# Queries of two units from a copy of the pixels, keys of two units in the other step, bias coefficients laid out contiguously

## The chip, the cores and the metric

The kernel runs on one NeuronCore of one Trainium2 chip. The metric is the device time of one execution in microseconds; the time given is the median of three runs. The kernel before takes 3091.45 us (3091.44 to 3092.21).

## The reference

The input is x, two images of 128 channels and 256 x 256 pixels, in fp32. Two layers follow each other, each adding its result to its input after a group normalisation.

Layer 0 is halo attention. Pixels are grouped in windows of 8 x 8; each window's 64 queries look at the 12 x 12 pixels around it. There are four heads of 32 channels:

```python
qkv = jnp.einsum('bchw,oc->bohw', x, W_qkv)
q = q * SCALE
attn = jnp.einsum('bnd,bmd->bnm', q, k)
attn = attn + rel_pos_emb(q, rel_height, rel_width) + FIXED_MASK
attn = jax.nn.softmax(attn, axis=-1)
out = jnp.einsum('bnm,bmd->bnd', attn, v)
return jnp.einsum('bchw,oc->bohw', out, W_out)
```

The fixed mask puts minus infinity on every pair of query and key whose row or column distance has the wrong parity. What is left is four separate attentions per window: 16 queries (4 x 4) against 36 keys (6 x 6) of one parity of rows and one of columns. The position terms are dot products of a query with a table, one per row distance and one per column distance. They are linear in the pixel, so they can be computed from the normalised pixels with the tables folded into the query weights.

Layer 1 is a pair of convolutions whose results are multiplied; the change doesn't touch it, except that one of its buffers is declared with the shape of a buffer of layer 0.

## The kernel before

Layer 0 works in strips of eight image rows, 32 strips an image, 64 in all. A strip k has two units u = 2k and 2k + 1, one for each parity r of rows; a unit holds both parities c of columns, 16 pairs of windows each. 128 units run one after the other in `attention_fast` (L548 to L597).

The normalised pixels of a strip are in `xn[k % 2]` (two buffers), by row parity, pair of windows, column parity and then a cell of 10 x 6 pixels (j rows, i columns) that belongs to one window of the pair and the halo. The name `by_cell` gives this view. `inner(k, r, c, lo, hi)` takes rows 1 to 8 of each cell and columns lo to hi of it: four floats, then a step to the next cell row, six floats further.

There is also a copy of the pixels by place, `xq`: one buffer, with the layout place column t2, half of the pairs, place row t1, r, pair n, c, e. POOL fills it in `by_place` (L331), eight copies a strip: four in the even unit of the strip before and four in the odd one. Only the bias coefficients read it.

What a unit does, in the order in which the code emits it:

- `normalise(k + 1)`, in even units: POOL copies the old columns (L312), VectorE normalises the new ones in four instructions (L321) and copies edges (L326, L327).
- `by_place` for half of strip k + 1's columns (L335, POOL), `old_keys(u + 1)` (L346, POOL): key columns that the next unit shares with the strip before.
- `biases(u)` (L447): 16 matmuls put the position terms and the mask into four PSUM banks `sc`, `scores(u)` (L463) adds query times key, and ScalarE takes the exponentials (L472).
- `values(u, j)` (L428): four tiles, evicted by ScalarE and VectorE into `vt` (L434).
- `coefficients(k + 1, r)` (L407): 16 matmuls from `xq` with the folded tables `wb`, evicted by ScalarE (L416) and VectorE (L420) into `cf`.
- `attend(u)` (L488): probabilities times values, 64 matmuls in three tiles, divided on VectorE (L494, L495).
- `turn(u)` (L506): two transposes on VectorE.
- `queries(u + 1)` and `keys(u + 1)`: two tiles each. A query tile of 512 columns reads `inner(k, r, c, 1, 5)`, cut into three matmuls by `in_parts`, and is evicted twice by ScalarE (L388), once for each parity of heads, into `q` (two buffers). A key tile reads `inner(k, r, c, 2, 6)`, is cut into two, and is evicted once by ScalarE (L363). In the first strip of an image a key unit has one tile more (`top`).
- `project(u)`: two tiles (L353 by `in_parts`, L522 on VectorE), and the DMA of the result on SP's queue.

All of these matmul tiles but `sc` share a pool of four PSUM banks (`pj`) in turn. The order on each engine is the order of the code: `tc.manual_schedule(engines=ORDERED)` leaves nothing to a planner. In the first unit, `queries(0)` and `keys(0)` are emitted before the first coefficients; in the last strip, steps of layer 1 are put where queries, keys and coefficients fall away.

Of the kernel before, what the change touches and what calls it, by code (L numbers as in the profile page):

```python
# [10 lines left out]
F32 = mybir.dt.float32  # L11
# [9 lines left out]
P = 128  # L21
# [4 lines left out]
SCALE = DH ** -0.5  # L26
NEG = -1.0e30
NPAIR = 16
XC = 131
XW = 272  # L30

# [135 lines left out]
def attention_fast(tc, io, x1_d, norm, st_x, st_y, tags, ends, weights, both, layer1):  # L167

    nc = tc.nc
# [4 lines left out]
    with ExitStack() as l0:  # L174
# [35 lines left out]
            for g in range(2)  # L210
        ]

        xq = both.sb.tile([P, 4, 2, 4, 2, 8, 2, 2], F32, tag="xq", name="f_xq")
        wb = both.sb.tile([P, 4, 4, HEADS, 16], F32, tag="wb", name="f_wb")
        for i in range(2):
            nc.gpsimd.memset(xn[i], 0.0)
# [77 lines left out]
        def inner(k, r, c, lo, hi):  # L294

            return by_cell(k)[:, r, c::2, 1:9, lo:hi]
# [34 lines left out]
        def by_place(k, columns):  # L331
            cells = by_cell(k)
            for t2 in columns:
                for half in range(2):
                    nc.gpsimd.tensor_copy(  # L335
                        xq[:, t2, half].rearrange("p t r n c e -> p r t (n c) e"),
                        cells[:, :, 16 * half : 16 * half + 16, 1 + t2 : 9 : 4, 1:5].rearrange(
                            "p r a e i -> p r i a e"
                        ),
                    )  # L340

        def old_keys(u):
            k, r = divmod(u, 2)
# [1 line left out]
                for c in range(2):  # L345
                    nc.gpsimd.tensor_copy(kt[r][k % 2][:, c, :, 0:2], kt[r][(k + 1) % 2][:, c, :, 4:6])  # L346

        def in_parts(count, dst, w, moving):


            cuts = [NPAIR * i // count for i in range(count + 1)]
            for lo, hi in zip(cuts, cuts[1:]):
                nc.tensor.matmul(dst[:, 32 * lo : 32 * hi], w, moving[:, lo:hi], start=True, stop=True)  # L353

        def keys(u):
            k, r = divmod(u, 2)
            s = k % NS
            cur = kt[r][k % 2]

            def part(c):  # L360
                pk = ps_pj.tile([P, 512], F32, tag="pj", name=f"f_pk_{u}_{c}")
                in_parts(2, pk, wkT, inner(k, r, c, 2, 6))
                nc.scalar.copy(cur[:, c, 1:129, 2:6], pk.rearrange("p (j i) -> p j i", i=4))  # L363

            def top():
# [12 lines left out]
        def queries(u):  # L378

            k, r = divmod(u, 2)  # L380
            q = wk.tile([P, 2, NPAIR, 2, 32], F32, tag="q", name=f"f_q_{u}")
            qs[u] = q

            def part(c):
                pq = ps_pj.tile([P, 512], F32, tag="pj", name=f"f_pq_{u}_{c}")
                in_parts(3 if u % (2 * NS) else 1, pq, wq_s, inner(k, r, c, 1, 5))
                for i in range(2):
                    nc.scalar.activation(  # L388
                        q[:, c, :, i], pq.rearrange("p (n x) -> p n x", n=NPAIR), AF.Copy,
                        scale=head[:, i : i + 1],  # L390
                    )

            return [lambda c=c: part(c) for c in range(2)]

        def coefficients(k, r):

            if r == 0:
                cfs[k] = wk.tile([P, 2, 2, 8, 2, 2, 16], F32, tag="cf", name=f"f_cf_{k}")
            pa = ps_pj.tile([P, 512], F32, tag="pj", name=f"f_pa_{k}_{r}")
            for t in range(8):
                t2, t1 = 2 * r + t // 4, t % 4
                for half in range(2):
                    nc.tensor.matmul(  # L407
                        pa[64 * half : 64 * half + 64, 64 * t : 64 * t + 64],
                        wb[:, t2, t1].rearrange("p h x -> p (h x)"),
                        xq[:, t2, half, t1].rearrange("p r n c e -> p (r n c e)"), start=True, stop=True,  # L410
                    )
            src = pa.rearrange("p (t m e) -> p e m t", t=8, e=2)
            for i in range(2):
                dst = cfs[k][..., i, 8 * r : 8 * r + 8].rearrange("p e r n c t -> p e (r n c) t")
                if i == 0:
                    nc.scalar.activation(  # L416
                        dst, src, AF.Identity, bias=keep[:, 1:2], scale=keep[:, 0:1]
                    )
                else:
                    nc.vector.tensor_scalar(  # L420
                        dst, src, keep[:, 2:3], keep[:, 3:4], ALU.mult, ALU.add
                    )
# [16 lines left out]
        def biases(u):  # L439

            k, r = divmod(u, 2)
            for e in range(2):
                for half in range(2):
                    for g in range(2):
                        rows = slice(64 * half + 32 * g, 64 * half + 32 * g + 32)
                        for c in range(2):
                            nc.tensor.matmul(  # L447
                                sc[g][half][64 * c : 64 * c + 64, :, :, 16 * e : 16 * e + 16].rearrange(
                                    "p n i x -> p (n i) x"
                                ),  # L450
                                hot[rows, e],
                                cfs[k][rows, e, r, :, c].rearrange("p n i x -> p n (i x)"),
                                start=e == 0, stop=False, skip_group_check=True,
                            )

# [59 lines left out]
        def project(u):  # L515
# [2 lines left out]
            x1s[u] = x1 = x1p.tile([P, 4, W], F32, tag="x1", name=f"f_x1_{u}")  # L518
            for c in range(2):
                py = ps_pj.tile([P, 512], F32, tag="pj", name=f"f_py_{u}_{c}")  # L520
                in_parts(2, py, woT, ots.pop((u, c)).rearrange("p (n x) -> p n x", n=NPAIR))
# [20 lines left out]
        with tc.manual_schedule(engines=ORDERED):  # L542
            normalise(0)
            by_place(0, range(4))
            emit(queries(0) + keys(0))
            coefficients(0, 0)
            coefficients(0, 1)
            for u in range(NU):  # L548
                k, r = divmod(u, 2)
                b, s = divmod(k, NS)  # L550
# [36 lines left out]
                    next(layer1)  # L587
                turn(u)
                step()
                if later:  # L590
                    emit(queries(u + 1) + keys(u + 1))
                step()
                if u > 0:
                    result_stats(u - 1)
# [30 lines left out]
def convolutions_fast(tc, io, x1_d, norm, st_y, out, weights, count_good, both):  # L625
# [4 lines left out]
    with ExitStack() as l1:  # L630
# [57 lines left out]
        def row_sums(k):  # L688
            s = k % NS
            xt = xn[k % 2]  # L690
            if k == 0:
                sm = both.sb.tile([P, 4, 2, 4, 2, 8, 2, 2], F32, tag="xq", name=f"sm_{k}")
# [828 lines left out]
```

## Time and profile before

| | |
|---|---|
| median of three runs | 3091.45 us |
| the profiled execution: its own time, its span | 3091.2 us, 3089.4 us |
| granted TensorE clock, mean | 0.998 of full |
| TensorE matmuls (PE), weight loads (PEld) | 2966.2 us busy (96%), 2247.5 us (73%) |
| VectorE (DVE), ScalarE (ACT), POOL | 2532.0 us (82%), 1710.0 us (55%), 571.3 us (18%) |
| queries: f_pq of 160 and of 192 columns | 1008 and 504 records |
| keys and projection: f_pk, f_py, 256 columns | 1024 and 1024 records |
| layer 0's units | from 108.03 us to about 2098 us of the span |

A page line for a group gives the line of the code, the engine, the operation, what it writes and reads, its shape, how many there are, the busy time and the mean length of one. Matmuls overlap: [...] the distance from start to start says what one costs. Each fp32 matmul of the code stands in the trace as two records. PE is the engine of the matmuls, and PEld its weight loads, which run beside them.

### The profile page before, as it was taken

Reading aid. Unit: us, or ns where it says so; the run is one execution under the profiler, and the core shown is the slowest. Engines: PE = TensorE matmul, PEld = TensorE weight load, DVE = VectorE, ACT = ScalarE, POOL = GpSimd, SP = SyncE. Lnnn points to the kernel's source line nnn. Section 1 sums busy time; section 2 is a strip of 40 time slices with the busy share of each in tenths; the row PEclk is TensorE's granted clock in tenths of the full one; section 3 lists DMA queues with packets and bytes.
Section 4 is the critical chain, followed back from the end, with each engine's and each line's share of the span. In section 5 each row is a group of like instructions: output and inputs, shape, how many; then the busy total and the mean of one; then the engine's idle time right before and its main releaser. Section 6 shows DMA issues by size and latency. Waiting matters only on the chain.

```text
span 3089.4 us, 116074 instructions
## 1 busy us (share of the span) xinstructions
PE 2966.2 (96%) x52006; PEld 2247.5 (73%) x52006; DVE 2532.0 (82%) x4092; ACT 1710.0 (55%) x2673; POOL 571.3 (18%) x921
## 2 busy tenths in 40 slices
PE   0799999999999999999999999999999999999998
PEld 0688888888889888998888899885444444444443
DVE  8788888888888877777777777778999999999998
ACT  0455555555555555555555555555666665666664
POOL 2222222222222222222222222220000000000001
PEclk9999999999999999999999999999999999999999
DMA  9433333333333221222222222235788888888886
GB/s 393 165 125 129 112 115 112 115 112 115 111 115 111 78 78 68 88 71 88 71 88 71 88 71 88 71 97 137 206 221 218 218 217 215 216 215 216 216 217 167
DMA packets 137400, 434.75 MB, mean 141 GB/s; under 512 B 12992, under 2 KB 87616, under 8 KB 104384
## 3 DMA queue, kind: packets, MB, share of 16 engines
q1 hardware_dynamic: 127824, 361.18, 33.7%
q0 software_dynamic: 9072, 66.06, 11.7%
q8 instruction: 412, 6.75, 0.9%
q14 instruction: 92, 0.75, 0.1%
HBM read 284.59 MB, written 134.22 MB: 136 GB/s over the span
## 4 chain that ended last, share of the span: by engine, by line
PE 93%; DVE 2%; ACT 1%; issue 0%; DMA 0%; SPq 0%; DVEq 0%; ACTq 0%
PE f_pv L428 15%; PE a_e L738 10%; PE a_o L738 10%; PE f_pq L353 9%; PE f_s L463 8%; PE f_o L488 8%; PE f_pk L353 7%; PE f_py L353 7%; PE f_pa L407 5%; PE f_s L447 4%; PE a_d L777 3%; PE b L817 2%; PE a_c L738 2%; PE g L718 2%; DVE f_xn L321 0%
## 5 line engine op out<-in xcount | busy, mean ns | idle before, releaser
L434 DVE COPY f_vt<-f_pv 64x512 f32<-64x512 f32 x512 | 354.5, 695 | 288.9 <-ACT f_vt L434 288.6
L428 PE MATMUL f_pv<-f_wqkvT,f_xn 128*128 128x128 f32 x4096 | 491.3, 278 | 0.0
L472 ACT ACTIVATE f_p<-f_s 128x512 f32<-128x512 f32 x512 | 264.3, 603 | 404.6 <-PE f_s L463 404.6
L388 ACT ACTIVATE f_q<-f_pq,f_head 128x512 f32<-128x512 f32 x512 | 309.8, 688 | 299.5 <-PE f_pq L353 299.5
L428 PEld LDWEIGHTS f_pv<-f_wqkvT,f_xn 128*128 128x128 f32 x4096 | 466.9, 192 | 8.6
L335 POOL COPY f_xq<-f_xn 128x256 f32<-128x256 f32 x512 | 311.7, 652 | 756.4 <-DVE f_xn L321 756.4
L434 ACT COPY f_vt<-f_pv 64x512 f32<-64x512 f32 x512 | 297.8, 583 | 117.6 <-PE f_pv L428 117.4
L799 ACT ACTIVATE t<-t,w 128x1024 f32<-128x1024 f32 x128 | 146.9, 1148 | 372.7 <-DVE t L794 367.9
L806 DVE SCALAR_TENSOR_TENSOR t<-t,w,t 128x1024 f32<-128x1024 f32 x256 | 329.9, 1289 | 7.5 <-ACT t L799 1.3
L463 PEld LDWEIGHTS f_s<-f_q,f_kt 64*64 64x64 f32 x16384 | 250.6, 135 | 49.2 <-issue 49.2
L353 PE MATMUL f_pq<-f_xn,f_wq_s 128*128 128x192 f32 (+2 forms) x1520 | 276.9, 329 | 3.3 <-DVE f_xn L321 2.6
L463 PE MATMUL f_s<-f_q,f_kt 64*64 64x64 f32 x16384 | 268.1, 220 | 0.0
L488 PE MATMUL f_o<-f_vt,f_p 128*32 128x66 f32 x16384 | 263.6, 222 | 1.0 <-DVE mean_x L132 0.4
L488 PEld LDWEIGHTS f_o<-f_vt,f_p 128*32 128x32 f32 x16384 | 241.9, 110 | 10.3 <-DVE f_cf L420 1.0
L353 PE MATMUL f_pk<-f_xn,f_wqkvT 128*128 128x256 f32 x1024 | 245.8, 380 | 0.0
L353 PEld LDWEIGHTS f_pq<-f_xn,f_wq_s 128*128 128x128 f32 x1520 | 232.4, 188 | 17.1 <-issue 4.2
L353 PE MATMUL f_py<-f_ot,f_woT 128*128 128x256 f32 x1024 | 241.8, 379 | 1.5 <-DVE f_ot L506 1.5
L738 PE MATMUL a_e<-xm,w1s 128*128 128x512 f32 x512 | 240.7, 591 | 0.0
L738 PE MATMUL a_o<-xm,w1s 128*128 128x512 f32 x512 | 240.3, 590 | 0.0
L312 POOL COPY f_xn<-f_xn 128x1280 f32<-128x1280 f32 x62 | 87.0, 1403 | 770.5 <-PE f_pv L428 770.5
L835 POOL DMA_DIRECT2D y<-f_x x63 | 54.5, 865 | 915.2 <-DVE y L827 900.2
L522 DVE TENSOR_TENSOR f_x<-f_py,f_raw 128x512 f32<-128x512 f32 x256 | 176.0, 688 | 57.5 <-PE f_py L353 49.2
(131 smaller groups left out, 4668.2 us busy)
## 6 DMA issues: line engine op xcount, KB each, us to landing
f_raw<-in_x SPq DMA_DIRECT2D x62, 1280.0 KB, 7.7
f_sx<-in_x SPq DMA_DIRECT2D x64, 1024.0 KB, 12.4
f_x<-f_x SPq DMA_DIRECT2D x128, 512.0 KB, 3.5
y<-f_x POOLq DMA_DIRECT2D x63, 1024.0 KB, 7.9
out<-y SPq DMA_DIRECT2D x63, 1024.0 KB, 4.3
raw<-f_x SPq DMA_DIRECT2D x64, 640.0 KB, 6.4
raw<-f_x SPq DMA_DIRECT2D x62, 384.0 KB, 5.9
t<-t4p SPq DMA_DIRECT2D x192, 32.0 KB, 4.7
```

The costliest lines, as they stand in the source:

```text
L335: nc.gpsimd.tensor_copy(xq[:, t2, half].rearrange("p t r n c e -> p r t (n c) e"), cells[:, :, 16 * half : 16 * half + 16, 1 + t2 : 9 : 4, ...
L353: nc.tensor.matmul(dst[:, 32 * lo : 32 * hi], w, moving[:, lo:hi], start=True, stop=True)
L388: nc.scalar.activation(q[:, c, :, i], pq.rearrange("p (n x) -> p n x", n=NPAIR), AF.Copy, scale=head[:, i : i + 1],)
L407: nc.tensor.matmul(pa[64 * half : 64 * half + 64, 64 * t : 64 * t + 64], wb[:, t2, t1].rearrange("p h x -> p (h x)"), xq[:, t2, half, t1]. ...
L428: nc.tensor.matmul(pv[:, P * n : P * n + P], xn[k % 2][:, r, 4 * j + n].rearrange("p c x -> p (c x)"), wvT, start=True, stop=True,)
L434: (nc.vector.tensor_copy if c else nc.scalar.copy)(vt[rows, 4 * j : 4 * j + 4, :, c, 0:32], pv[rows].rearrange("p (n h d) -> p n h d", n=4 ...
L463: nc.tensor.matmul(sc[g][n // 8][64 * c : 64 * c + 64, n % 8].rearrange("p i x -> p (i x)"), keys_k[rows, c, 48 * n : 48 * n + 64], qs[u][ ...
L472: nc.scalar.activation(pts[u][:, g, 8 * half : 8 * half + 8].rearrange("p n i x -> p (n i x)"), sc[g][half].rearrange("p n i x -> p (n i x ...
L488: nc.tensor.matmul(po[32 * h : 32 * h + 32, n - lo], p[:, h // 2, n, h % 2], vt[:, n, h], start=True, stop=True,)
L522: nc.vector.tensor_tensor(x1[:, :, c:W:2], py.rearrange("p (m t) -> p t m", t=4), raws[k][:, r:8:2, c:W:2], ALU.add,)
L738: nc.tensor.matmul(pa[:, : n * W], w, rows, start=i == 0, stop=i == len(terms) - 1)
L806: nc.vector.scalar_tensor_tensor(t3[:, j : j + 4], t1[:, j + tap : j + tap + 4, :], w3[:, tap : tap + 1], t3[:, j : j + 4], ALU.mult, ALU.add,
```

## The change

Four things are changed together.

The copy by place has another order: half, t2, t1, r, c, n, e. For given half, row parity r and column parity c, each of the 16 places (t2, t1) has 16 contiguous floats. `by_place` needs twice as many copies on POOL, each half as large.

The queries read this copy instead of the cells: 16 runs of 16 floats for each half of a tile. The output of such a matmul is written so that `pq` holds the same order as before: its columns go to PSUM with a step of 16 floats, and the runs one float apart. So the queries of a strip can be computed only when the whole copy of that strip is there. They are emitted for both units of the next strip in the odd unit, four tiles one after another; even units get the keys of the next unit and the one after it, also four tiles.

The cuts are no longer a count but a list: `TWO` cuts a tile in halves, `THREE` leaves the first half and cuts the second in quarters, `ONE` doesn't cut. Which tiles get which depends on the unit.

The coefficients `cf` have the order e, r, c, n, i, place: what one bias matmul reads is one run of 256 floats, where it was eight runs of 32.

Before the first unit, the keys of unit 0 come first, then the coefficients, then the queries of units 0 and 1.

```diff
+ONE, TWO, THREE = (0, 32), (0, 16, 32), (0, 16, 24, 32)
...
-        xq = both.sb.tile([P, 4, 2, 4, 2, 8, 2, 2], F32, tag="xq", name="f_xq")
+        xq = both.sb.tile([P, 2, 4, 4, 2, 2, 8, 2], F32, tag="xq", name="f_xq")
...
                 for half in range(2):
-                    nc.gpsimd.tensor_copy(
-                        xq[:, t2, half].rearrange("p t r n c e -> p r t (n c) e"),
-                        cells[:, :, 16 * half : 16 * half + 16, 1 + t2 : 9 : 4, 1:5].rearrange(
-                            "p r a e i -> p r i a e"
-                        ),
-                    )
+                    for c in range(2):
+                        nc.gpsimd.tensor_copy(
+                            xq[:, half, t2, :, :, c].rearrange("p t r n e -> p r t n e"),
+                            cells[
+                                :, :, 16 * half + c : 16 * half + 16 : 2, 1 + t2 : 9 : 4, 1:5
+                            ].rearrange("p r n e i -> p r i n e"),
+                        )
...
-        def in_parts(count, dst, w, moving):
-            cuts = [NPAIR * i // count for i in range(count + 1)]
+        def in_parts(cuts, dst, w, moving):
+            last, n = cuts[-1], moving.shape[1]
             for lo, hi in zip(cuts, cuts[1:]):
-                nc.tensor.matmul(dst[:, 32 * lo : 32 * hi], w, moving[:, lo:hi], start=True, stop=True)
+                nc.tensor.matmul(
+                    dst[:, 512 * lo // last : 512 * hi // last], w,
+                    moving[:, n * lo // last : n * hi // last], start=True, stop=True,
+                )
-        def keys(u):
+        def keys(u, first=TWO, second=TWO):
...
-                in_parts(2, pk, wkT, inner(k, r, c, 2, 6))
+                in_parts(second if c else first, pk, wkT, inner(k, r, c, 2, 6))
...
-        def queries(u):
+        def queries(u, first, second):
...
-                in_parts(3 if u % (2 * NS) else 1, pq, wq_s, inner(k, r, c, 1, 5))
+                cuts = second if c else first
+                for lo, hi in zip(cuts, cuts[1:]):
+                    half, lo, hi = lo // 16, lo % 16, (hi - 1) % 16 + 1
+                    nc.tensor.matmul(
+                        pq.rearrange("p (h n e t) -> p h t n e", h=2, n=8, e=2)[:, half, lo:hi], wq_s,
+                        xq[:, half, :, :, r, c].rearrange("p s t n e -> p (s t) n e")[:, lo:hi],
+                        start=True, stop=True,
+                    )
...
-                cfs[k] = wk.tile([P, 2, 2, 8, 2, 2, 16], F32, tag="cf", name=f"f_cf_{k}")
+                cfs[k] = wk.tile([P, 2, 2, 2, 8, 2, 16], F32, tag="cf", name=f"f_cf_{k}")
...
-                                cfs[k][rows, e, r, :, c].rearrange("p n i x -> p n (i x)"),
+                                cfs[k][rows, e, r, c].rearrange("p n i x -> p n (i x)"),
...
-            emit(queries(0) + keys(0))
+            emit(keys(0, ONE, TWO))
             coefficients(0, 0)
             coefficients(0, 1)
+            for u in range(2):
+                emit(queries(u, TWO, TWO))
...
-                if later:
-                    emit(queries(u + 1) + keys(u + 1))
+                if r == 0:
+                    top = s == 0 or (k + 1) % NS == 0
+                    if u == 0:
+                        emit(keys(1, ONE, ONE))
+                    else:
+                        emit(keys(u + 1, TWO if top else THREE))
+                    if more:
+                        emit(keys(u + 2, TWO if top else THREE))
+                elif later:
+                    second = THREE if k % 4 else TWO
+                    emit(queries(u + 1, THREE, TWO) + queries(u + 2, THREE, second))
```

The matmuls of the coefficients read the same 64 floats as before in the new order, and their evictions write `cf` in the new order, with the same runs of eight floats. The projection keeps its two halves.

More of the change, by code (lines that the diff above doesn't have):

```diff
@@ L409, in coefficients @@
                         wb[:, t2, t1].rearrange("p h x -> p (h x)"),
-                        xq[:, t2, half, t1].rearrange("p r n c e -> p (r n c e)"), start=True, stop=True,
+                        xq[:, half, t2, t1].rearrange("p r c n e -> p (r c n e)"), start=True, stop=True,
                     )
@@ L413, in coefficients @@
             for i in range(2):
-                dst = cfs[k][..., i, 8 * r : 8 * r + 8].rearrange("p e r n c t -> p e (r n c) t")
+                dst = cfs[k][..., i, 8 * r : 8 * r + 8].rearrange("p e r c n t -> p e (r c n) t")
                 if i == 0:
@@ L520, in project @@
                 py = ps_pj.tile([P, 512], F32, tag="pj", name=f"f_py_{u}_{c}")
-                in_parts(2, py, woT, ots.pop((u, c)).rearrange("p (n x) -> p n x", n=NPAIR))
+                in_parts(TWO, py, woT, ots.pop((u, c)).rearrange("p (n x) -> p n x", n=NPAIR))
                 nc.vector.tensor_tensor(
@@ L691, in row_sums @@
             if k == 0:
-                sm = both.sb.tile([P, 4, 2, 4, 2, 8, 2, 2], F32, tag="xq", name=f"sm_{k}")
+                sm = both.sb.tile([P, 2, 4, 4, 2, 2, 8, 2], F32, tag="xq", name=f"sm_{k}")
                 sm = sm.rearrange("p a b c d e g h -> p (a b c d e g h)").rearrange(
```

## The prediction

> **What bounds the kernel now.** I read the page first: busy shares, then the chain that ended last.
>
> ```profile
> PE 2966.2 (96%) x52006; PEld 2247.5 (73%) x52006; DVE 2532.0 (82%) x4092; ACT 1710.0 (55%) x2673; POOL 571.3 (18%) x921
> ...
> PE 93%; DVE 2%; ACT 1%; issue 0%; DMA 0%; SPq 0%; DVEq 0%; ACTq 0%
> ```
>
> TensorE holds 93% of the chain. Of the waits only one group in layer 0's steady part stops it, and only three times: the bias coefficients. The release it is put down to was long over; their data come from POOL's pixel copy.
>
> ```profile
> engine line waited for: us in total, times, longest us
> PE pm_x L129 <- issue: 87.0, 1, 87.0
> ...
> PE f_pa L407 <- DVE f_vt L434: 5.0, 3, 3.9
> ```
>
> The timeline of TensorE over one unit (start, length) has no idle entry at all, and the next unit repeats it 15.47 us later:
>
> ```profile
> 1005.25 2.05 PE L488 MATMUL f_o<-f_vt,f_p 128*32 128x66 f32 x128
> 1007.23 2.15 PE L353 MATMUL f_pq<-f_xn,f_wq_s 128*128 128x160 f32 x12
> 1009.22 1.92 PE L353 MATMUL f_pk<-f_xn,f_wqkvT 128*128 128x256 f32 x8
> 1010.98 1.89 PE L353 MATMUL f_py<-f_ot,f_woT 128*128 128x256 f32 x8
> 1012.80 1.12 PE L447 MATMUL f_s<-f_cf,f_hot 32*64 32x256 f32 x32
> ```
>
> So time is the sum of the matmuls' own prices, as long as nobody is late for TensorE. Every matmul of the program stands as two records. Two tiles of queries take 1.99 us (1007.23 to 1009.22), two of keys 1.76. Start to start, one record each, from the trace: queries of 160 columns 147.6 ns, of 192 columns 177.0; keys of 256 columns 220.1; the contiguous f_py of 256 columns 215.6; f_pv of 128 columns 111.6. The first record after a change of array shape costs 104 ns more, before and after alike.
>
> [...] queries read runs of four floats[...], 0.91 ns a column (slope between 160 columns at 147.6 and the few of 512 at 468); keys begin on 8 bytes, 0.85; f_py reads contiguously, 0.83. [...] No matmul of the kernel before scatters its output: the nearest, the biases, writes runs of 16 floats with gaps and runs at the price of contiguous output (a round of eight concurrent 256-column records every 215.6 ns). [...] Queue q8 agrees (6.75 MB in 412 packets), and a steady unit has exactly 768 instructions of TensorE, three blocks.
>
> **The change, part by part.**
>
> *Queries.* Before, a tile is cut in 160, 160 and 192 columns: 4 x 147.6 + 2 x 177.0 = 944 ns. After, moving data come in aligned runs of 16 floats, so I read them at f_py's price: two halves of 256 are 4 x 215.6 = 862; a half and two quarters 2 x 215.6 + 4 x 111.6 = 878. Three strips in four have three tiles of 878 and one of 862, the fourth two and two: 3491 ns a strip against 4 x 944 = 3778.
> *Keys.* Four tiles of 4 x 220.1 = 880, 3522 a strip; after, two of them are cut in three (2 x 220.1 + 4 x 111.6 = 887): 3534.
> Sum per strip 7025 against 7299: 274 ns less. For the 63 strips after the first: 17.2 us.
> *The scattered output.* This is the unknown: each query column now lands 64 bytes from the one before. Low end: nothing[...]. It cannot be below nothing, contiguous output being what f_py has. [...] In between lies what ScalarE pays for reading this PSUM layout with a step of 64 floats: f_cf 778 ns against 582 for a contiguous f_vt, some 0.38 ns an element, 195 ns a tile. I take nothing[...].
> *Biases.* Their moving data were runs of 32 floats, already at 215.6 a round: contiguous data give 0.
> *Pixel copy on POOL.* Twice the copies, half the elements, in the same order of columns. In an even unit:
>
> ```profile
> 1016.49 2.49 POOL L335 COPY f_xq<-f_xn 128x256 f32<-128x256 f32 x4 [10.78 <-DVE f_xn L321]
> 1018.93 0.77 POOL L346 COPY f_kt<-f_kt 128x262 f32<-128x262 f32 x2
> 1019.65 2.38 POOL L335 COPY f_xq<-f_xn 128x256 f32<-128x256 f32 x4
> ```
>
> A copy is 0.58 to 0.64 us. Half of it would be 0.31; a fixed cost of 0.11 us (from L346's 0.38 for 262 elements and L312's 1.40 for 1280) makes it 0.35 to 0.38; I take 0.37. Eight end at 1016.5 + 3.0 = 1019.5. The coefficients on TensorE start at 1019.64 and need the last four copies only halfway, at 1020.2; TensorE reaches that point some 0.15 us earlier after the change. Cover of 0.5 us; from 0.42 us a copy on it is gone. What follows on POOL (old keys, then the odd unit's copies) is needed a unit later. Units 4, 8, 62 and 70, where this wait already shows, get some 0.3 us worse each: +1.
> *Moves.* Even units now have four key tiles between heads and projection, odd units four query tiles: 3.5 us, against 3.65 before. The projection needs VectorE's first transpose, done 2.5 us after the queries' start, so it stays covered. ScalarE evicts four query tiles in 8 x 0.6 = 4.8 us; the fourth key or query tile's bank is wanted by the next values 8 us after the start; both query buffers are free since the scores of this unit and the previous one are over. Scores need the first two tiles alone. ScalarE's exponentials, queued behind the evictions, begin only at 7.7 us. No DMA is issued otherwise or moved past.
> *Start.*
>
> ```profile
> 100.56 4.91 POOL L335 COPY f_xq<-f_xn 128x256 f32<-128x256 f32 x8 [81.29 <-DVE f_xn L321]
> ...
> 104.19 2.09 PE L407 MATMUL f_pa<-f_xq,f_wb 128*64 128x64 f32 x64
> ...
> 108.03 1.12 PE L447 MATMUL f_s<-f_cf,f_hot 32*64 32x256 f32 x32 [1.75 <-DVE f_cf L420]
> ```
>
> Queries used to fill the time of POOL's copy; now they wait for it. 16 copies of 0.37 end at 106.5, coefficients at 106.9, four query tiles at 110.4; biases start some 2.5 us later than 108.03. ScalarE then still has four evictions and its table load (1.28 us) ahead of the first exponentials, at 114.2; the heads end about 121.0 instead of 117.9. With the keys of two units behind them, unit 1 starts 3.1 us late, but with 1.76 us of strip 1's keys done: net +1.3.
> *End.* In unit 126 no queries stand between heads and projection: keys are 1.86, the transpose comes at 2.5, so a stall of 0.7.
> Sum: -17.2 + 1.3 + 0.7 + 1 = -14.2 us. The profiled execution took 3091.2 (span 3089.4, 1.8 around it), the median is 3091.45: 3077.2 for an execution like the profiled one, 3077.3 by the median.
>
> **Rivals.**
> *The scattered output costs (slower).* Place: the query matmuls of odd units. It decides from 14.2 / 256 tiles = 55 ns a tile, 6% of its price. [...] at ScalarE's ratio +50, so 3127. For it: [...] ScalarE's 778 against 582. Against it: [...] the biases' gaps at no price.
> *POOL becomes late.* With 0.45 us a copy, the last lands 0.25 us after its need in each of 63 even units: +16, so 3093. For it: a cover of half a microsecond, and L335's slower copies beside VectorE's L327. Against it: L346's small fixed cost.
> *The instruction stream drifts off its 768 a unit.* The cuts in three or two change the count by 4 to 8 a unit; if blocks then end inside the dense bursts, each such unit may lose what unit 126 shows, 0.26 us of idle "issue" inside f_o: up to 127 x 0.26 = 33, of which I take half, 3094. Against it: stretches of the trace before with offsets 6 and 14 apart have no stall.
>
> **How the numbers follow.** Gain as summed: 0.74, itself within 3070 to 3084 (copies, start and quarter pieces uncertain by some us each). Late POOL 0.06, instruction stream 0.04, both near 3093. Scattered output 0.16[...]. The time given is that of the first case, 3077. The range 3069 to 3099 takes in the first three cases, 0.8 to 0.84, and leaves out the last. No change, within 0.2% (6 us, about what a measurement of this kernel can tell), is 3085 to 3098. Faster: the first case and no other, 0.74. Same: the middle two, most of them, 0.08. Slower: 0.18.
>
> **What would show it.** Right: f_pq records of 256 columns 215 to 217 ns apart; steady even plus odd unit 30.67 us instead of 30.95; no new wait of f_pa in even units; unit 1 starting near 127.5 us. Wrong: f_pq records 270 ns or more apart (scatter); f_pa waiting in every even unit (POOL); gaps ended by "issue" inside f_o or f_s (instructions). A keys tile that waits for a bank would overthrow the paragraph on moves.

## The result, and the profile after

The kernel with the change takes 3078.0 us (median of six runs, 3077.57 to 3078.61) where the kernel before took 3091.72 (six runs, 3091.44 to 3094.49): a ratio of 0.9953, 95% interval 0.9943 to 0.9964. The prediction's 3077 is 1 us off. The profiled execution took 3077.89, its span is 3076.0, 13.4 us shorter than before.

The page of the changed kernel: busy shares, and shares of the chain that ended last.

```profile
PE 2950.9 (96%) x52090; PEld 2223.8 (72%) x52090; DVE 2522.4 (82%) x4092; ACT 1732.8 (56%) x2673; POOL 657.8 (21%) x1433
...
PE 93%; DVE 2%; ACT 1%; issue 0%; POOL 0%; DMA 0%; SPq 0%; DVEq 0%; ACTq 0%
```

TensorE still holds 93% of the chain; POOL is 86 us busier, and that has not become the bound. In the lines below `f_pa` are the coefficients, `f_s` biases and scores, `f_o` probabilities times values, and "issue" is idle time in which an engine waited for nothing that the profile shows. TensorE's waits in the changed kernel (us in total, times, longest):

```profile
PE f_pa L418 <- DVE f_vt L445: 5.3, 4, 2.9
...
PE f_py L354 <- DVE f_ot L517: 2.2, 2, 1.5
...
PE f_pa L418 <- POOL f_xq L337: 1.4, 4, 0.4
...
PE f_o L499 <- issue: 0.7, 1, 0.7
PE f_s L474 <- issue: 0.6, 1, 0.6
```

The coefficients wait 6.7 us in all (5.0 before): 0.7 us ahead of the first unit, for POOL's copy, and 6.0 in units 4, 8, 62 and 70, but in no regular even unit. New are a wait for the transpose in the tail and two short idle times that end by "issue". TensorE's timeline over an odd unit's end and the even unit after it (start, length):

```profile
1000.79 3.75 PE L393 MATMUL f_pq<-f_xq,f_wq_s 128*128 128x256 f32 x20
1004.38 1.89 PE L354 MATMUL f_py<-f_ot,f_woT 128*128 128x256 f32 x8
1006.20 1.12 PE L458 MATMUL f_s<-f_cf,f_hot 32*64 32x256 f32 x32
...
1016.10 3.79 PE L354 MATMUL f_pk<-f_xn,f_wqkvT 128*128 128x256 f32 x20
1019.73 1.89 PE L354 MATMUL f_py<-f_ot,f_woT 128*128 128x256 f32 x8
1021.54 1.12 PE L458 MATMUL f_s<-f_cf,f_hot 32*64 32x256 f32 x32
```

Four query tiles take 3.59 us start to start (1000.79 to 1004.38), four key tiles 3.63 (1016.10 to 1019.73); the even unit is 15.34 us long (1006.20 to 1021.54), against 15.47 before, with no idle entry. POOL in the same unit:

```profile
1009.24 3.39 POOL L337 COPY f_xq<-f_xn 128x128 f32<-128x128 f32 x8 [9.97 <-DVE f_xn L322]
```

The eight copies for the coefficients end at 1012.63; TensorE starts the coefficients at 1013.04 and needs the last four copies halfway, near 1013.6.

### The profile page after: what moved, and what is told of

The parts are those of the page before. It is cut to its first block, busy times and chain, and to the rows that moved or that the text cites. A ratio compares the mean times of both kernels' runs of the same rounds, so it can differ in the third digit from the quotient of the medians.

```text
span 3076.0 us, 116627 instructions
## 1 busy us (share of the span) xinstructions
PE 2950.9 (96%) x52090; PEld 2223.8 (72%) x52090; DVE 2522.4 (82%) x4092; ACT 1732.8 (56%) x2673; POOL 657.8 (21%) x1433
## 4 chain that ended last, share of the span: by engine, by line
PE 93%; DVE 2%; ACT 1%; issue 0%; POOL 0%; DMA 0%; SPq 0%; DVEq 0%; ACTq 0%
PE f_pv L439 15%; PE a_e L760 10%; PE a_o L760 10%; PE f_s L474 8%; PE f_o L499 8%; PE f_pk L354 8%; PE f_pq L393 7%; PE f_py L354 7%; PE f_pa L418 4%; PE f_s L458 4%; PE a_d L799 3%; PE b L839 2%; PE a_c L760 2%; PE g L740 2%; POOL f_xq L337 0%
## 5 line engine op out<-in xcount | busy, mean ns | idle before, releaser
L337 POOL COPY f_xq<-f_xn 128x128 f32<-128x128 f32 x1024 | 399.2, 441 | 707.9 <-DVE f_xn L322 647.9
L399 ACT ACTIVATE f_q<-f_pq,f_head 128x512 f32<-128x512 f32 x512 | 303.1, 703 | 145.2 <-PE f_pq L393 145.2
L367 ACT COPY f_kt<-f_pk 128x512 f32<-128x512 f32 x256 | 154.6, 604 | 196.4 <-PE f_pk L354 196.4
L354 PE MATMUL f_pk<-f_xn,f_wqkvT 128*128 128x256 f32 (+2 forms) x1258 | 243.0, 345 | 0.0
L393 PE MATMUL f_pq<-f_xq,f_wq_s 128*128 128x256 f32 (+1 forms) x1370 | 240.5, 331 | 0.8 <-DVE f_rc L505 0.8
L393 PEld LDWEIGHTS f_pq<-f_xq,f_wq_s 128*128 128x128 f32 x1370 | 208.2, 191 | 23.3 <-PE pv_x L141 0.4
```

The costliest lines, as they stand in the source:

```text
L337: nc.gpsimd.tensor_copy(xq[:, half, t2, :, :, c].rearrange("p t r n e -> p r t n e"), cells[:, :, 16 * half + c : 16 * half + 16 : 2, 1 + ...
L354: nc.tensor.matmul(dst[:, 512 * lo // last : 512 * hi // last], w, moving[:, n * lo // last : n * hi // last], start=True, stop=True,)
L393: nc.tensor.matmul(pq.rearrange("p (h n e t) -> p h t n e", h=2, n=8, e=2)[:, half, lo:hi], wq_s, xq[:, half, :, :, r, c].rearrange("p s t ...
L399: nc.scalar.activation(q[:, c, :, i], pq.rearrange("p (n x) -> p n x", n=NPAIR), AF.Copy, scale=head[:, i : i + 1],)
```

## The experiments

Each ratio is to the kernel before, run beside it; its median stayed between 3091.94 and 3092.22. "Steady unit" is the median distance from one unit's biases to the next one's.

### The price of the read: queries from the cells again

The changed kernel with the same order of work, the same cuts and the pixel copy still made, but with the query matmuls reading the cells as before (and so writing contiguously).

```diff
-                for lo, hi in zip(cuts, cuts[1:]):
-                    ...
-                        xq[:, half, :, :, r, c].rearrange("p s t n e -> p (s t) n e")[:, lo:hi],
-                    ...
+                in_parts(cuts, pq, wq_s, inner(k, r, c, 1, 5))
```

> The changed kernel, but queries read the cells again (four floats at an odd place) and write PSUM contiguously; order, cuts, POOL copies and coefficients stay as changed. Theory (the read price is the gain): 256 columns cost 0.91 ns x 256 + 2 = 235 ns a record instead of 216, a tile in halves 940 instead of 863, in three pieces 944 instead of 876; 283 ns a strip, 63 strips: +18 us on the changed kernel, 3096, so a little above the kernel before. Rival (the new order of queries and keys brings the gain, the read little): stays within 4 us of the changed kernel, 3078 to 3082.

3094.7 us (3093.0 to 3096.15), ratio 1.0006 [0.9997, 1.0015]: 16.7 us more than the changed kernel. Odd units, where the queries stand, are 15.598 us instead of 15.324; even units are unchanged. The groups of this kernel, split by shape (records, busy us, mean ns of one):

```profile
L354 PE MATMUL f_pq<-f_xn,f_wq_s 128*128 128x256 f32 x678 | 196.7, 406 | 0.8 <-DVE f_rc L499 0.8
L354 PE MATMUL f_pq<-f_xn,f_wq_s 128*128 128x128 f32 x692 | 109.8, 279 | 0.0
```

and of the changed kernel:

```profile
L393 PE MATMUL f_pq<-f_xq,f_wq_s 128*128 128x256 f32 x678 | 184.3, 389 | 0.8 <-DVE f_rc L505 0.8
L393 PE MATMUL f_pq<-f_xq,f_wq_s 128*128 128x128 f32 x692 | 105.1, 274 | 0.0
```

The same counts and shapes, a shorter record; what the two kernels differ in besides, the order of the output, the next experiment tries alone. All else that the change does (other cuts, other order, doubled copies) gains nothing without the read.

### The price of the scattered output

The changed kernel with the query matmuls writing contiguously. The queries of a window then stand in another order in `pq`, so what is computed is not the same attention.

```diff
-                        pq.rearrange("p (h n e t) -> p h t n e", h=2, n=8, e=2)[:, half, lo:hi], wq_s,
+                        pq[:, 256 * half + 16 * lo : 256 * half + 16 * hi], wq_s,
```

> The changed kernel, but a query matmul writes its columns to PSUM one beside the other, not 16 floats apart; the queries of a window then stand in another order, so the result is not the reference's. Theory (scattered fp32 output is free): within 1 us of the changed kernel, 3078, and 216 ns from record to record at 256 columns, 111 at 128. Rival (the scatter costs something, and the read gains more than it shows): 3078 less 256 tiles x its price; 10 ns a tile would show as 2.6 us.

3077.64 us (3075.92 to 3078.18), ratio 0.995 [0.9934, 0.9967]. Steady units are 15.343 and 15.324 us, to the nanosecond those of the changed kernel, and 256-column query records start 215 to 216 ns apart in both. A step of 16 floats between columns costs an fp32 matmul nothing here.

### Run length or alignment?

The kernel before, with one edit: queries read the same runs of four floats, two floats further on, as the keys do. They begin on a multiple of 8 bytes instead of at 4 or 12 in every 16. Queries are then those of other pixels.

```diff
-                in_parts(3 if u % (2 * NS) else 1, pq, wq_s, inner(k, r, c, 1, 5))
+                in_parts(3 if u % (2 * NS) else 1, pq, wq_s, inner(k, r, c, 2, 6))
```

> The kernel before, but queries read columns 2 to 5 of each cell instead of 1 to 4: still runs of four floats, now on 8 bytes, as the keys do. The queries are of other pixels, so the result is not the reference's. Theory [...]: 0.86 ns a column as for keys, 160 columns 138 ns instead of 147.6, 192 columns 166 instead of 177, a tile 884 instead of 944: -15 us, 3076. Rival (short runs cost, wherever they begin): no change, 3091.

3079.0 us (3078.41 to 3080.57), ratio 0.9955 [0.9939, 0.9972]; steady units 15.367 instead of 15.473. The query groups of the kernel before, by shape:

```profile
L353 PE MATMUL f_pq<-f_xn,f_wq_s 128*128 128x160 f32 x1008 | 202.4, 321 | 0.8 <-DVE f_rc L494 0.8
L353 PE MATMUL f_pq<-f_xn,f_wq_s 128*128 128x192 f32 x504 | 129.7, 338 | 0.0
```

and with the shifted read:

```profile
L353 PE MATMUL f_pq<-f_xn,f_wq_s 128*128 128x160 f32 x1008 | 194.1, 313 | 0.8 <-DVE f_rc L494 0.8
L353 PE MATMUL f_pq<-f_xn,f_wq_s 128*128 128x192 f32 x504 | 124.4, 327 | 0.0
```

So most of the gain is where a run begins, not its length. Over the units without an irregularity, scaled to 126 of them, the shift saves 13.5 us and the change 17.9. The remaining quarter is left for the longer runs: other cuts and order are worth nothing in the steady units, since two of them together take 30.94 us in the changed kernel that reads the cells and 30.95 in the kernel before. The measured prices, 0.91 and 0.86 ns a column, are what the traces show; why the first byte of a run matters, they do not.

### Biases, coefficients and pixel copy without the queries

The kernel before with the new order of `cf` and of the pixel copy (16 smaller copies a strip) and nothing else; the coefficients read the copy in its new order.

```diff
-        xq = both.sb.tile([P, 4, 2, 4, 2, 8, 2, 2], F32, tag="xq", name="f_xq")
+        xq = both.sb.tile([P, 4, 2, 4, 2, 2, 8, 2], F32, tag="xq", name="f_xq")
...
-                cfs[k] = wk.tile([P, 2, 2, 8, 2, 2, 16], F32, tag="cf", name=f"f_cf_{k}")
+                cfs[k] = wk.tile([P, 2, 2, 2, 8, 2, 16], F32, tag="cf", name=f"f_cf_{k}")
...
```

> The kernel before with the new order of the coefficients and of the pixel copy (twice as many copies on POOL) alone; queries and keys as before. Theory (bias matmuls are at their price already, POOL's copies are covered): 0 to +1.5 us on the kernel before, 3092 to 3093, with the coefficients waiting only in the units in which they wait now. Rival (contiguous coefficients save reading, or POOL's 16 copies a strip come late in every even unit): -3 us or less, or +10 us or more.

3090.47 us (3089.17 to 3093.41), ratio 0.9995 [0.9986, 1.0004]: no difference that can be told, and steady units of 15.473 us, those of the kernel before. The contiguous biases are worth nothing that shows, and the doubled copies cost nothing that shows.

### How much cover POOL's copy has

The changed kernel with the first four copies of every even unit made twice.

```diff
-            for t2 in columns:
+            for t2 in (0, 0, 1) if columns == (0, 1) else columns:
```

> The changed kernel with POOL's first four pixel copies of every even unit made twice (unit 0's own at the start aside): 4 x 0.414 = 1.66 us more on POOL ahead of the coefficients, 63 times, nothing else. Theory, from the trace of the changed kernel: its copies end at 1012.55 and the half that needs the last four starts at 1013.58, a cover of 1.03 us, so coefficients wait 0.6 us in each even unit: 63 x 0.6 = 40 us more, 3118 us, with some 60 waits of f_pa put down to POOL's f_xq. Rival, the prediction's cover (0.5 us): 1.16 us each, 73 us, 3151. Second rival: the stall is taken back inside the unit by other waits, or POOL starts its copies earlier than VectorE's last normalisation: under 20 us, below 3098.

3110.41 us (3109.19 to 3113.24), ratio 1.0059 [1.0044, 1.0075]: 32.4 us more than the changed kernel. Even units are 15.876 instead of 15.343 us, 0.53 each; 60 of them make 32. POOL and TensorE in one such unit, from their timelines:

```profile
1022.52 4.70 POOL L337 COPY f_xq<-f_xn 128x128 f32<-128x128 f32 x12 [10.00 <-DVE f_xn L322]
```

```profile
1026.30 0.80 PE L418 MATMUL f_pa<-f_xq,f_wb 128*64 128x64 f32 x18
1027.28 0.68 PE L418 MATMUL f_pa<-f_xq,f_wb 128*64 128x64 f32 x14 [0.19 <-POOL f_xq L337]
```

Twelve copies end at 1027.22; the second half of the coefficients goes on 0.06 later. (The 0.19 in brackets is counted from the modelled end of the matmul before; what the wait costs is read from the length of the unit.) From the unit's start, the last copy for the coefficients ends 1.34 us later than in the changed kernel (1027.22 - 1019.45 against 1012.63 - 1006.20), less than the 1.66 that I counted, and 0.53 of that comes through. So the cover is 0.8 us: less than the 1.03 that I read from the timeline (where I had taken 1012.55, the start of the next entry, for the copies' end at 1012.63), more than the 0.5 that the prediction gave it. The rival "POOL becomes late" was real, and 0.8 us away.

### The instruction stream: the same pieces everywhere

All tiles of 256 + 128 + 128 columns cut in halves instead, in the changed kernel. A unit then has 758 or 759 instructions of TensorE instead of 766 to 770. A block is here what one packet of queue q8, the queue of instructions, brings: the trace of the changed kernel has 412 packets of 16 KiB on it, and in layer 0 TensorE starts 256 instructions from one packet to the next in the mean (256.2 over 379 distances, 255.7 over 380 in the kernel before).

```diff
-ONE, TWO, THREE = (0, 32), (0, 16, 32), (0, 16, 24, 32)
+ONE, TWO, THREE = (0, 32), (0, 16, 32), (0, 16, 32)
```

> The changed kernel with every list of three pieces replaced by halves, so that TensorE has some 19 instructions less in each pair of units. Theory (a block of 256 instructions may begin anywhere): tiles in halves are 12 ns cheaper for queries and 4 for keys, 42 ns a strip: -2.6 us, 3075.5. Rival (the pieces keep the count at 1536 a pair, so that blocks begin in quiet places): idle time that ends by issue of 0.3 to 0.7 us inside f_o or f_s in a third or more of the units as the blocks wander, +10 us or more, 3088.

3126.39 us (3123.82 to 3129.65), ratio 1.0107 [1.009, 1.0123]: 48.4 us more than the changed kernel, where I had expected 2.6 less. The undisturbed units are in fact cheaper (15.341 and 15.279 us). TensorE's waits in this kernel:

```profile
PE f_o L499 <- issue: 25.4, 47, 1.8
PE f_s L474 <- issue: 7.4, 12, 1.0
```

The list counts from modelled ends of matmuls and so too little. Summing the distances from each record to the next inside a burst (the 128 records in a row of one unit), f_o has 41.2 us more than in the changed kernel and f_s 9.6: 50.8 of the 51.8 us that this profiled execution, at 3129.65 the slowest of four, is longer.

Counting TensorE's instructions through the trace gives the place. Of the 63 gaps over 0.3 us between two records of a burst, 62 sit at number 193 or 194 within a block of 256, and the matmuls go on 2.2 to 2.9 us after the transfer of a block begins on queue q8. The changed kernel has 6144 instructions in eight units, exactly 24 blocks, so number 193 recurs in the same matmuls. Here it wanders through all places of the unit.

That it falls into a burst isn't enough. In the changed kernel it does so in every undisturbed unit, 2.3 us into the unit in f_s and 8.2 in f_o, as in the kernel before, and TensorE doesn't stop. In these two kernels the last transfer on q8 had begun at least 2.3 us earlier, mostly more than 3. So the traces point to transfers that begin too late for the place at which TensorE needs them; what sets when one begins, they don't show.

### The same count, shifted

The changed kernel, with 45 small matmuls on a spare tile ahead of the first normalisation: 180 instructions more, all at the start.

```diff
+            pad = ps_pj.tile([P, 512], F32, tag="pj", name="f_pad")
+            for i in range(45):
+                nc.tensor.matmul(
+                    pad[0:32, 0:64], hot[:, 0, 0:32], hot[:, 1], start=True, stop=True
+                )
             normalise(0)
```

> The changed kernel with 45 small matmuls into an unused bank while TensorE waits for the first statistics: no time of their own, but 180 instructions more ahead of the first unit, so that every block of 256 begins 76 instructions later in its unit than now. Theory (where the blocks begin in the unit decides): the offset of units 9 and 10 of the all-halves kernel, which are 1.1 and 1.4 us longer than its quiet ones, now in every unit: +90 to +170 us, near 3215, all of it idle time ended by issue in f_o and f_s. Rival (the halves themselves or their drift cost, not the place of the blocks): 3078, as the units are unchanged.

3200.35 us (3196.55 to 3202.25), ratio 1.0347 [1.033, 1.0365]: 122 us more for work that fits into time in which TensorE idled anyway. Its waits:

```profile
PE f_s L474 <- issue: 49.6, 105, 1.1
PE f_o L499 <- issue: 26.6, 44, 1.4
```

Inside the f_s bursts 80.0 us are added from record to record, inside f_o 42.9: together all of it. The clock isn't the cause: the mean granted clock is 0.984 here and 0.998 in the changed kernel, but the half clock lies ahead of the first unit, and from 100 us on it is 1.00 in every stretch of 500 to 800 us. Number 193 now falls 0.7 us into each unit, at the biases, and near 3.4 us in f_s and 10 in f_o. The 256 instructions up to the second of these are mostly the dense f_s, a little over 2 us of work, and again TensorE goes on 2.2 to 2.9 us after a transfer began. In the kernels before and after, a block's number 193 in these bursts costs nothing that shows: ahead of the last strip no two records of a burst start 0.25 us apart there. In these two it is 0.3 to 1.8 us wherever it shows in a list of waits.

### Other pieces, the same count

The three-piece cut moved from the keys and queries to the projection; nearly the same number of instructions a unit.

```diff
-                        emit(keys(u + 1, TWO if top else THREE))
+                        emit(keys(u + 1))
...
-                    emit(queries(u + 1, THREE, TWO) + queries(u + 2, THREE, second))
+                    emit(queries(u + 1, TWO, TWO) + queries(u + 2, TWO, second))
...
-                in_parts(TWO, py, woT, ...)
+                in_parts(TWO if ... else THREE, py, woT, ...)
```

> The changed kernel with queries and keys in halves but the projection's tiles cut in three pieces instead, so that a pair of units keeps its 1536 instructions; the last queries keep their pieces three times in four. Theory (the pieces only fill the count): as the changed kernel within 2 us, 3078, with no idle time ended by issue in the steady part. Rival (queries in halves are bad where they stand): near the all-halves kernel, 3126.

3078.88 us (3077.44 to 3081.01), ratio 0.9958 [0.9944, 0.9972], the changed kernel's time within the scatter of both. Which of these tiles are cut makes no difference that can be told; how many instructions a unit has does.

### The start, and the weights' sums, in one kernel

Unit 0's and 1's queries read from the cells while POOL copies, VectorE's sums of layer 1's weights moved from unit 8 to unit 71, and seven small matmuls ahead to move the block boundaries by 28 instructions.

```diff
...
+            for i in range(7):
+                nc.tensor.matmul(pad[0:32, 0:64], hot[:, 0, 0:32], hot[:, 1], start=True, stop=True)
...
+            for u in range(2):
+                emit(queries(u, TWO, TWO, copied=False))
             emit(keys(0, ONE, TWO))
             coefficients(0, 0)
             coefficients(0, 1)
-            for u in range(2):
-                emit(queries(u, TWO, TWO))
...
-                if u == 8:
+                if u == 71:
                     weights.sums()
```

> The changed kernel with three repairs: queries of units 0 and 1 from the cells, ahead of the first coefficients; the sums of layer 1's weights on VectorE in unit 71 instead of 8, where VectorE has no input statistics; seven small matmuls at the start, so that blocks begin 28 instructions earlier in the unit. Theory: start -2.5, unit 8 -3.7 (it comes to unit 4's excess of 0.8), the two idle times by issue in units 126 and 127 -1.0: 3071. Rival (the start is bound by POOL's copies alone, and the blocks' new place is worse): 3074 or more.

3121.6 us (3120.79 to 3123.18), ratio 1.0094 [1.0077, 1.0111]: 50 us away from what I expected. Two things went wrong. The start gained nothing: unit 1 begins at 127.06 us instead of 126.94, since the first query tiles run slowly there, 16 records in 5.7 us, 358 ns each where 0.91 ns a column, the price in steady units, makes about 235, and push the coefficients to 106.7. And the pad moved number 193 to about 11 us into the unit, into the query or key tiles right after f_o. Up to about unit 60 that is nearly free; the norms add a few matmuls in units 61 and 69, which bring it to 10.3 to 10.9, and from unit 70 on it stalls in nearly every unit. Two of the waits:

```profile
PE f_pq L395 <- issue: 5.3, 15, 0.6
PE f_pk L354 <- issue: 4.1, 4, 2.4
```

So these idle times are not bound to the small matmuls: here they stand in tiles of 128 and 256 columns, behind a burst. In unit 8 the wait of the coefficients fell to 0.73 us, as expected, but the idle time of 2.4 us in its key tiles took most of the gain back. Three edits in one kernel hid what each is worth, so the sums were moved alone.

### The sums alone

```diff
-                if u == 8:
+                if u == 71:
                     weights.sums()
```

> The changed kernel with VectorE's six sums of layer 1's weights moved from unit 8 to unit 71, and nothing else; the same instructions on TensorE in the same places. Theory: in unit 8 the sums stand ahead of the strip's normalisation on VectorE, the pixel copy starts late and the bias coefficients wait, 4.6 us over the steady unit against 0.8 in unit 4, which has the statistics alone; unit 71 is odd, its coefficients were copied a unit earlier, so VectorE's delay of some 5 us is swallowed there. Unit 8 falls by 3.7 us: 3074.3 us, and the f_pa waits named after f_vt lose their longest entry of 2.9 us. Rival: VectorE's backlog in unit 71 makes its evictions of values late for TensorE, or unit 8's wait has another cause: 3077 to 3080.

3074.02 us (3073.61 to 3074.26), ratio 0.994 [0.9927, 0.9954]. Unit 8 has 0.85 us over the steady unit instead of 4.55, unit 71 is unchanged. TensorE in unit 8 of the changed kernel:

```profile
244.93 1.88 PE L418 MATMUL f_pa<-f_xq,f_wb 128*64 128x64 f32 x32 [2.95 <-DVE f_vt L445]
246.74 2.86 PE L499 MATMUL f_o<-f_vt,f_p 128*32 128x66 f32 x128
```

and of this one:

```profile
242.57 1.15 PE L418 MATMUL f_pa<-f_xq,f_wb 128*64 128x64 f32 x32 [0.78 <-DVE f_vt L445]
243.65 2.05 PE L499 MATMUL f_o<-f_vt,f_p 128*32 128x66 f32 x128
```

The wait is 2.2 us shorter. The other 1.5 of the 3.7 us, which I had not counted apart, are the two groups behind it: 1.81 and 2.79 us to the next start in the changed kernel, 1.08 and 1.98 here. There the granted clock is at half from 245.1 to 248.5 us, right after the wait; here it stays full. The kernel before has the same half clock in unit 8, 3.4 us from 244.1. The wait alone doesn't bring it on: with the doubled copies unit 8 waits 3.25 us and keeps the full clock. So 2.2 us are the wait that I had in mind; the rest came with the edit too, but why the half clock is gone stays open.

### What is queued on ScalarE: the root of the norm

As the kernel with the sums in unit 71, and in units 61 and 69 the square root of a norm stands between the evictions of the two units' queries.

```diff
-                    emit(queries(u + 1, THREE, TWO) + queries(u + 2, THREE, second))
-                step()
+                    emit(queries(u + 1, THREE, TWO))
+                    step()
+                    emit(queries(u + 2, THREE, second))
+                if u not in norm_at:
+                    step()
```

> As the kernel with the weight sums in unit 71 (3074.0 us), and in units 61 and 69 ScalarE's square root of the norm stands after the evictions of two query tiles instead of all four. Theory: the changed kernel put four query tiles (eight evictions, 4.74 us) where two query and two key tiles (3.55 us) stood ahead of that root, so VectorE's reciprocal of it comes 1.16 us later (1.88 us after the next unit's start instead of 0.72), and with it the normalisation, the pixel copy and the coefficients of units 62 and 70, 2.2 and 1.1 us over what they were. With the root 2.37 us earlier units 62 and 70 fall from 18.15 and 16.58 us to 16.0 and 15.5: 3.3 us, 3070.8. Rival: the pixel copy alone (twice the copies) makes these units late, or the later evictions come too late for a bank: no gain, 3073.5 to 3076.

3071.81 us (3071.53 to 3072.4), ratio 0.9933 [0.9919, 0.9946], 2.2 us below the one without it. ScalarE in unit 61 of the changed kernel:

```profile
1064.68 4.74 ACT L399 ACTIVATE f_q<-f_pq,f_head 128x512 f32<-128x512 f32 x8 [3.53 <-PE f_pq L393]
...
1070.72 0.20 ACT L147 ACTIVATE sd_x<-v_x 128x1 f32<-128x1 f32 x1
```

and of this one:

```profile
1061.06 2.42 ACT L399 ACTIVATE f_q<-f_pq,f_head 128x512 f32<-128x512 f32 x4 [3.52 <-PE f_pq L393]
...
1064.80 0.20 ACT L147 ACTIVATE sd_x<-v_x 128x1 f32<-128x1 f32 x1
```

The root comes 6.04 us after the first eviction starts in the one, 3.74 in the other. VectorE's reciprocal of it starts 1.88 us after unit 62's start in the changed kernel and 0.72 here, as in the kernel before. Unit 70 falls by 1.11 us and is what it was before the change (0.13 over the steady unit), unit 62 by 1.09. I had expected 2.1 of unit 62: I had not seen that 0.86 of its excess is work, the extra key tile of a new image's first strip, which the change moved from unit 63 (0.86 over the steady unit before, 0.00 after) to unit 62.

This is the fastest kernel of the study, 3071.8 us against 3078.0 with the change alone.

## Why the prediction was right

The sum, part by part, from the starts of the 128 units in both traces. The steady part is the mean saving of the 117 units without an irregularity, 0.1423 us, times 126.

| part | predicted, us | measured, us |
|---|---|---|
| reads of queries and keys, 126 units | -17.2 | -17.93 |
| start (+1.3) and end (+0.7) | +2.0 | +3.06 |
| units that wait for coefficients | +1 | +1.47 |
| sum | -14.2 | -13.40 |

*Queries and keys.* A steady even plus odd unit was to be 30.67 us and is 15.343 + 15.324 = 30.67; the query records of 256 columns were to start 215 to 217 ns apart and start 215 apart. The step "read at f_py's price" is confirmed by putting the old read back (+16.7 us), and the alignment behind three quarters of it by shifting the read alone.

*Scattered output.* I took nothing, and nothing is what the contiguous output shows: 3077.64 us against 3078.0. Why it costs nothing is not shown by any run. For this rival the trace showed only ScalarE's 778 ns against 582, a read of PSUM; the rest of the 0.16 given to it was an estimate of mine.

*Biases.* Zero, as predicted, by the kernel that changes them alone.

*Pixel copy.* Mis-sized twice, in opposite directions. A copy takes 0.414 us beside VectorE's work (3.31 us for eight) and not 0.37, since the fixed cost was read from copies of another form. The cover is 0.8 us and not 0.5: POOL now begins 3.04 us after the biases, where it began 3.69 after them before, because the first of its smaller copies can start while VectorE's last normalising instruction still runs. I had kept the old start, 1016.5. By my own numbers 0.42 was the brink; the copies all but reached it, with 0.8 us still in hand. The sum for this rival was wrong too: eight copies of 0.45 us are 0.64 us longer than eight of 0.37, which a cover of 0.5 leaves 0.14 us late, 9 us in all and not the 16 that I gave.

*Units that wait.* The net came out near the +1 predicted, but not from the four units named alike. Units 4 and 8 improved (-0.1 and -0.9, POOL's earlier start). Units 62 and 63 together lost 1.3 and unit 70 1.1. The paragraph on moves failed here: it counted the evictions of four query tiles on ScalarE and looked for who wants the exponentials, and left out the norm's square root, which in two units is queued behind these evictions and ahead of VectorE's normalisation. That is 1.1 us in each, shown by moving the root.

*Start.* The timeline of TensorE at the start of the changed kernel:

```profile
106.80 3.72 PE L393 MATMUL f_pq<-f_xq,f_wq_s 128*128 128x256 f32 x16
110.45 1.12 PE L458 MATMUL f_s<-f_cf,f_hot 32*64 32x256 f32 x32
...
126.94 1.12 PE L458 MATMUL f_s<-f_cf,f_hot 32*64 32x256 f32 x32
```

Coefficients were to end at 106.9 and end at 106.8, the query tiles at 110.4 and the biases start at 110.45. Unit 1 starts 2.56 us later than before, not 3.1; less the 1.76 us of keys done ahead, the start cost 0.8 and not 1.3.

*End.* The transpose makes the projection of unit 126 wait 0.70 us, as predicted. Not predicted were 0.73 us of "issue" inside f_o of unit 126 (0.26 before) and 0.56 inside f_s of unit 127 (none before), both at number 193 or 194 of a block: +1.0 by the list, and about 1.3 from start to start. So the end cost some 2.3 us and not 0.7, and the row is only 1.1 off because the start was 0.5 better. Their timeline:

```profile
2065.14 1.37 PE L499 MATMUL f_o<-f_vt,f_p 128*32 128x66 f32 x81 [0.73 <-issue]
...
2074.74 0.33 PE L474 MATMUL f_s<-f_q,f_kt 64*64 64x64 f32 x3 [0.56 <-issue]
```

*The rival of the instruction stream* was given 0.04 and at most 33 us. It didn't come, but the argument against it was poor. I had taken "the cuts change the count by 4 to 8 a unit" for a drift without adding it up over the strips: the units have 766 to 770 instructions, and eight of them 6144, 24 whole blocks. So there was no drift to allow for. Nor was a block's end inside a dense burst the danger that I took it for: number 193 lay in f_s and f_o in the kernel before already. And had there been a drift, 48 us was at stake, and 122 for a bad offset, enough to turn the gain into a loss. That it didn't come was luck: the right sign rested here on a sum that I had not made.

## What to carry to other kernels

Where a matmul's moving data are short runs, ask first on what byte a run begins: shifting runs of four fp32 from odd floats to even ones was worth 13 us of 3092 here, and making them four times as long some 4 us more in the steady units. Where dense small matmuls fill the time, count TensorE's instructions per loop body and keep the body at whole blocks of 256, at an offset that has been tried: an edit that removes work can cost nearly twenty times what it saves (48 us against 2.6). When evictions are moved on an engine, list all that stands behind them in that engine's order, also what appears in only a few iterations.

## What the runs showed that I had not expected

- An idle time of TensorE at number 193 or 194 of a block of 256 instructions, 0.3 to 2.4 us each in the lists of waits, in or just behind a burst of 64- or 66-column matmuls, where TensorE went on 2.2 to 2.9 us after the block's transfer on q8 began: 48 us in all for the kernel whose blocks drift, 122 us for the one with 180 instructions more ahead, of some 3100. The changed kernel has that number in both bursts of every steady unit (2.3 and 8.2 us in), and two such idle times in the whole of layer 0.
- A half clock of 3.4 us in unit 8, worth 1.5 us, in the kernels before and after alike, that is gone when VectorE's sums stand elsewhere.
- A step of 64 bytes between the output columns of an fp32 matmul costs nothing: 215 ns a record of 256 columns either way.
- The tail of layer 0 is where both kernels leave the steady count, and both lose some tenths of a microsecond there to "issue".
